# A masked update added to DRAM by accumulating transfers in the two cellular layers of a four-layer convolution kernel

## The chip, the cores and the metric

The kernel runs on one core of one Trainium2 chip. The metric is the device time of one execution in microseconds (us), lower is better. Three timed executions of the kernel before the change took 2888.09, 2889.95 and 2891.01 us; their median is 2889.95 us.

## The reference, cut to what matters

The input is 1024 samples of a 16 x 16 grid with 16 channels. Four layers follow each other, each of the form x = x + layer(groupnorm(x)). Layer 0 is a tensor-train product, layer 2 a 3 x 3 convolution. Layers 1 and 3, which the change touches, are one step of a cellular automaton:

```python
def update(x):                       # x is the normalized input
    xt = jnp.transpose(x, (0, 3, 2, 1))
    pre = _alive(xt)                 # channel 3, maximum over 3 x 3, > 0.1
    p = jnp.concatenate([xt, depthwise(xt, conv1), depthwise(xt, conv2)], axis=1)
    flat = p.reshape(B * W * Hh, 48)
    h = jax.nn.relu(flat @ fc0_w.T + fc0_b)          # 128 hidden values
    d = (h @ fc1_w.T + fc1_b).reshape(B, C, W, Hh)
    mask = (pre & _alive(d)).astype(xn.dtype)
    return jnp.transpose((xt + d) * mask, (0, 3, 2, 1))
x = x + update(_gn(x))               # _gn: group norm of 8 groups
```

So layers 1 and 3 need, for every element, x + (normalized x + d) * mask.

## The kernel before, in words

**Data.** The samples are worked on in two halves of 512 (n = 0 and 1). Two SBUF tiles, X0 and X1 (`XN`), hold one half each, as 128 partitions x 32 lines x 512 samples. Between layers a half lies in DRAM, in a tensor of its own per layer boundary: `xf[l][n]` (lines 117 to 122; `xf[3]` is another name of `xf[2]`).

**Passes.** A layer is done half by half. `layer_nca` (line 1461) is called four times, in this order on the chip: layer 1 half 0 (from 1662 us of the profile), layer 1 half 1 (from 1927 us), then, after the two convolution passes of layer 2, layer 3 half 0 (from 2376 us) and layer 3 half 1 (from 2627 us). I call these passes 1 to 4. While TensorE works on one half, VectorE normalizes the other half in the background (`norm_cw`, `norm_lines`: the lines 641, 649, 657, 669 and 682 in the profile).

**Inside a pass.** Both depthwise convolutions and the first matrix are folded into one product. One *row tile* is the 128 hidden values of one of 256 rows for 512 samples: several matmuls of 32 partitions into a PSUM bank `ph` (`tile_of_row`, line 1681, matmul on line 1704), then ScalarE's relu into an SBUF tile `hid` (line 1707). Four row tiles make a quad; two quads make one output tile of 128 partitions x 512 samples (`fc1`, line 1527, matmul on line 1534, PSUM bank `po`). There are 64 quads and 32 output tiles in a pass, eight output tiles in each of four quarters (q = 0 to 3). Then `finish` (line 1540) lets VectorE form u = po + bias + normalized x (line 1546), which also frees the bank `po`.

**Mask.** The mask is made in the first quarter alone, from flags of channel 3 (lines 1542 and 1564), by bf16 matmuls into two more banks (`pcnt`, line 1573) and two VectorE operations (lines 1578 and 1579). `masked` runs three slots after the `finish` of the following tile. In the later quarters the mask is there and `residual` (line 1583) follows `finish` directly.

**Residual.** `fetch` (line 1513) loads the old activations of the tile from DRAM into `r` on SyncE's DMA queue (SP). GpSimd (POOL) multiplies u by the mask (line 1587) and adds it to r (line 1588); for the last tile of a pass, and for tiles done in half width, VectorE does both. Seven slots later SP stores r to `xf[l + 1]` (line 1590). In pass 4 the sum is not stored but turned by TensorE (line 1598) and copied by VectorE into the output's layout.

**Order.** The order of instructions on every engine is the program's order. `plan` (line 1627) writes TensorE's order by hand, in slots. In a slot each of four groups of 32 partitions advances its own row tile by one matmul, so up to four matmuls run side by side; two quads that are complete take two slots. `room` (line 1636) lets a new row tile begin only if fewer than `BANKS` = 8 PSUM banks are taken in the plan; `pcnt` banks are not in that count, although they come from the same pool of eight (`nca_ps = dict(h=8)`, line 1857). `run` (line 1717) mixes loads and background steps between the slots. SBUF pools are given by `nca_sb` (line 1856): ten `hid` buffers, two of u, four of r.

Of the kernel before, what the change touches and what calls it, by code (L numbers as in the profile page):

```python
# [9 lines left out]
F32 = mybir.dt.float32  # L10
# [3 lines left out]
ALU = mybir.AluOpType  # L14
# [5 lines left out]
B, S, C = 1024, 16, 16  # L20
P = 128
NB = 512
NCH = B // NB
# [81 lines left out]
def conv_preact_kernel(ctx: ExitStack, tc: tile.TileContext, a: dict, out: bass.AP):  # L105
# [8 lines left out]

    XN = [big.tile([P, NL, NB], F32, tag=f"xn{i}", name=f"xn{i}") for i in range(2)]

    xf = [
        [dram.tile([8, 4, P, NB], F32, tag=f"xf{l}_{n}", name=f"xf{l}_{n}") for n in range(NCH)]
        for l in range(5)
    ]  # L120

    xf[3] = xf[2]

    xr = [dram.tile([2, S, P, NB], F32, tag=f"xr{n}", name=f"xr{n}") for n in range(NCH)]

# [762 lines left out]
    def tile_cw(t, i):  # L888

        return t[i % 8, i // 8]  # L890

    def rows_wc(t, wh, h, n=1):

        t = t[4 * wh : 4 * wh + 4].rearrange("w q (c h) b -> (w q c) h b", h=S)
        return t[:, h : h + n]
# [246 lines left out]
    def residual_steps(n, vs):  # L1142

        def add(w):
            G.dma_start(
                xf[1][n][w // 2].rearrange("q (c v h) b -> v (q c) h b", v=2, h=S)[w % 2],
                xr[n][w // 8, :, 16 * (w % 8) : 16 * (w % 8) + 16].rearrange("h f b -> f h b"),
                accum_op=ALU.add,
            )

        return [(1, lambda w=w: add(w)) for w in vs]

    def output_steps(n):

        steps = []

        lines = xf[4][n].rearrange("w q (c v h) b -> h (q c v) w b", v=2, h=S)

        def load(h, st):
            st["x"] = work([P, 8, P], "xs", "xs")
            for g in range(4):
                nc.sync.dma_start(st["x"][32 * g : 32 * g + 32], lines[h][:, :, P * g : P * g + P])

        def turn(h, st):
            st["o"] = work([P, 4, S, S], "xo", "xo")
            x = st["x"].rearrange("p w (j f) -> p f w j", f=4)
            for f in range(4):
                V.transpose(  # L1170
                    st["o"][:, f].rearrange("p (w v) c -> p w c v", v=2), x[:, f]
                )

        def store(h, st):
            nc.sync.dma_start(
                out[n * NB : n * NB + NB, h].rearrange("(p f) w c -> p f (w c)", f=4),
                st["o"].rearrange("p f w c -> p f (w c)"),
            )

        sts = [{} for _ in range(S)]  # L1180
        steps += [lambda: load(0, sts[0]), 4]
        for h in range(S):
            if h + 1 < S:
                steps.append((0, lambda h=h: load(h + 1, sts[h + 1])))
            steps += [lambda h=h: turn(h, sts[h]), (0, lambda h=h: store(h, sts[h]))]
        return steps
# [4 lines left out]
    def layer_train():  # L1191
# [78 lines left out]
        def tiles(t, a2, q, w):  # L1270

            return t[4 * a2 + w : 4 * a2 + w + 3 : 2, q].rearrange("w p b -> p w b")

        def store(u):
            ph, q, w = units[u]
            r = st["r", u]
            goes = OUTER[ph][1]
            if -1 in goes.values():
                neg = work([P, 2, NB], "t4", "neg")
                A.mul(neg, r, -1.0)  # L1280
            for (a2, n), sign in goes.items():
                first = all((a2, n) not in OUTER[j][1] for j in range(ph))
                src = r if sign > 0 else neg
                if first:
                    nc.sync.dma_start(tiles(xf[1][n], a2, q, w), src)
                else:
                    G.dma_start(tiles(xf[1][n], a2, q, w), src, accum_op=ALU.add)  # L1287

        def pieces(u, k):

# [73 lines left out]
    def layer_conv(X, n, other):  # L1364
# [75 lines left out]
        def finish(h):  # L1440

            if h == 0:
                G.tensor_copy(come, other[0:1, NL - 1, 0:1])
            for wh in range(2):
                r = work([P, NB], "r", "conv")
                A.activation(r, st["po", h][wh], AF.Identity, bias=b2)  # L1446
                G.dma_start(rows_wc(xf[2][n], wh, h), r.unsqueeze(1), accum_op=ALU.add)  # L1447

        steps = []
        for h in range(0, S, 2):  # L1450
# [10 lines left out]
    def layer_nca(X, n, l, L, xo=None):  # L1461
# [9 lines left out]
        def cols(hf):  # L1471
            return slice(0, NB) if hf is None else slice(hf * NB // 2, (hf + 1) * NB // 2)
# [39 lines left out]

        def fetch(i):
            r = st["r", *divmod(i, 8)] = work([P, NB], "r", "res1")
            nc.sync.dma_start(r, tile_cw(xf[l][n], i))

        def start():
            if n == 0 or l == 3:
# [8 lines left out]
        def fc1(q, w2, v, hf, hid):  # L1527
            if v == 0:
                st["po"] = bank([P, NB], "h", "po1")[:, width(hf)]
                if q > 0 and hf != 1:  # L1530
                    fetch(8 * q + w2)
            po = st["po"]
            for j in range(4):
                T.matmul(  # L1534
                    po[32 * j : 32 * j + 32], nca["w1"][:, v], hid[j], start=v == 0, stop=v == 1
                )
            if v == 1:
                finish(q, w2, hf, po)

        def finish(q, w2, hf, po):  # L1540
            if q == 0:
                V.tensor_scalar(
                    st["f", w2][64:96], po[96:128], nca["b1"][96:128], ALIVE, ALU.add, ALU.is_gt
                )
            u = st["u", q, w2] = work([P, NB], "u", "u")[:, width(hf)]
            V.scalar_tensor_tensor(u, po, nca["b1"], X[:, 8 * q + w2, cols(hf)], ALU.add, ALU.add)  # L1546
            if q > 0:
                residual(q, w2, hf)
                return

            ws = range(w2 - 1 if w2 else 0, 8 if w2 == 7 else w2)

            def masked():
                for w in ws:
                    mask(w)
                    residual(0, w)

            for w in ws:
                fetch(w)
            after(3, masked)  # L1560

        def flags(w2):
# [18 lines left out]
            )  # L1581

        def residual(q, w2, hf=None):
            u, r = st["u", q, w2], st["r", q, w2][:, cols(hf)]

            by = V if (q, w2) == (3, 7) or hf is not None else G
            by.tensor_tensor(u, u, st["m"][:, w2, cols(hf)], ALU.mult)  # L1587
            by.tensor_tensor(r, r, u, ALU.add)  # L1588
            if xo is None:
                after(7, lambda: nc.sync.dma_start(tile_cw(xf[l + 1][n], 8 * q + w2), r))  # L1590
            else:
                after(8 if hf is None else 4, lambda: turn(q, w2, r, hf))

        def turn(q, w2, r, hf):
            g0, n = (0, 4) if hf is None else (2 * hf, 2)
# [28 lines left out]
        def after(n, fn):  # L1624
            later.append((st["slot"] + n, fn))

        def plan():
# [6 lines left out]
            now, evacs, free_at, t, f = [None] * 4, 0.0, [], 0, 0  # L1634

            def room():
                return len(free_at) + sum(x is not None for x in now) < BANKS

            while f < len(quads):
                free_at = [b for b in free_at if b > t]  # L1640
# [110 lines left out]
    def put(L):  # L1751
        return lambda: nc.sync.dma_start(pack, L["pack"])
# [4 lines left out]
    def steps_of(*more):  # L1757
        return (lambda: None), [x for m in more for x in m]
# [14 lines left out]
    with ExitStack() as es:  # L1773
# [43 lines left out]
        def with_operand(i, step):  # L1817
# [31 lines left out]
        nst, N = parts_cw(X0, True, 3)  # L1849
        bg = alone(N, 0) + alone(N, 1) + alone(N, 2) + rstd(nst, slice(0, 96)) + [3] + scaled(N, range(3))  # L1850
        run(
            steps_of(phases[6]), 210, load_cw(X0, xf[1][0]) + [put(L1)], (bg, 0.12, 0.97), by=0.2
        )
    nst.clear()
    last = alone(N, 3) + rstd(nst, slice(96, 128)) + [3] + scaled(N, [3])
    nca_sb = dict(t4=2, s=3, n=2, wq=5, mask=1, f=5, hid=10, u=2, r=4, nx=1)
    nca_ps = dict(h=8)
    conv_sb, conv_ps = dict(gn, s=3, r=16, hx=2), dict(o=6, m=2)
    on_vector[0] = True
    with ExitStack() as es:  # L1860
        shared[0] = "h"
        stage(es, nca_sb, nca_ps)
        run(
            layer_nca(X0, 0, 1, L1), 250, load_cw(X1, xf[1][1]), (last, 0.0, 0.21),
            (norm_cw(X1, False), 0.23, 1.0), by=0.3,
        )
        run(
            layer_nca(X1, 1, 1, L1), 245, load_wc(X0, xf[2][0]), (norm_lines(X0, False), 0.2, 1.0), by=0.3
        )
    with ExitStack() as es:  # L1870
        shared[0] = "m"
        stage(es, conv_sb, conv_ps)
        (first0, main0), (first1, main1) = layer_conv(X0, 0, X1), layer_conv(X1, 1, X0)
        bg = norm_lines(X1)

        bg = bg[:-16] + woven(bg[-16:], *[(6 + i, copy) for i, copy in enumerate(first1)])
        run((lambda: now(first0), main0), 108, load_wc(X1, xf[2][1]), (bg, 0.09, 1.04), by=0.07)
        run(
            (lambda: None, main1), 108, load_cw(X0, xf[3][0]) + [put(L3)], (norm_cw(X0, True), 0.12, 1.06), by=0.07
        )  # L1880
    with ExitStack() as es:
        shared[0] = "h"
        stage(es, nca_sb, nca_ps)
        run(layer_nca(X0, 0, 3, L3), 245, load_cw(X1, xf[3][1]), (norm_cw(X1, False), 0.2, 1.0), by=0.3)
    with ExitStack() as es:
        stage(es, dict(nca_sb, xs=2, xo=2), nca_ps)

        xo = X0.rearrange("p n b -> p (n b)").rearrange("p (g h w c) -> p g h w c", g=4, h=S, w=S)
        run(layer_nca(X1, 1, 3, L3, xo), 280, (), (output_steps(0), 0.0, 0.93))
# [28 lines left out]
```

## Time and profile before

| what | value |
|---|---|
| three timed runs, median (lowest to highest) | 2889.95 us (2888.09 to 2891.01) |
| the profiled execution's own time | 2891.76 us |
| its span, from the first to the last instruction | 2890.1 us |
| TensorE (PE) busy | 2790.4 us, 97% of the span |
| VectorE (DVE) / ScalarE (ACT) / GpSimd (POOL) busy | 57% / 43% / 27% |
| pass 1, pass 2, pass 3, pass 4 begin | 1662, 1927, 2376, 2627 us |

The profile is one execution with every instruction's start and duration. A group of instructions is given by line, engine, operation and operands. "Idle before" is the time in which the engine stood still ahead of such an instruction, with the instruction whose end released it behind an arrow. PE is matmuls, PEld the loading of their weights, which overlaps them. Matmuls are pipelined, so a busy PE need not be at its peak. PEclk is the clock granted to TensorE as a share of the full one. TensorE takes an fp32 matmul as two records in the trace.

### The profile page before, as it was taken

What the parts mean: (1) busy time and instruction counts of PE and PEld (TensorE: products, weight loads), DVE (VectorE), ACT (ScalarE), POOL (GpSimd) and SP (SyncE); (2) the same over time, 40 slices, a digit from 0 to 9 for tenths busy, and PEclk for the clock granted to TensorE, in tenths of its full rate; (3) what the DMA queues carried; (4) which work ended last, traced back from release to release, by engine and by line L of the source; (5) the groups of instructions that cost most, each with busy time, mean ns of one, the idle gap of its engine ahead of it and who ended that gap; (6) DMA issues with size and microseconds to landing.
All of it is one profiled execution on the core that took longest, in us unless ns stands there. A gap on an engine that the chain in (4) does not pass through costs nothing.

```text
span 2890.1 us, 47471 instructions
## 1 busy us (share of the span) xinstructions
PE 2790.4 (97%) x19028; PEld 1831.6 (63%) x19028; DVE 1648.7 (57%) x1941; ACT 1237.2 (43%) x2168; POOL 773.4 (27%) x825
## 2 busy tenths in 40 slices
PE   5999999999999999999999999999999999999997
PEld 4777888877888888888888733333333334334443
DVE  7425744732644455444356568766977776857433
ACT  3243232124221211221122166676677666666664
POOL 1272010155012041000100015434542224443331
PEclk7899999999999999999999989999999999999998
DMA  6265744446485477363352154346447866444566
GB/s 231 82 128 182 255 131 140 125 78 155 116 221 103 91 179 178 77 156 63 81 142 38 22 168 155 123 139 208 133 127 183 194 93 224 135 127 123 146 191 214
DMA packets 261835, 408.58 MB, mean 141 GB/s; under 512 B 31828, under 2 KB 142984, under 8 KB 255472
## 3 DMA queue, kind: packets, MB, share of 16 engines
q1 hardware_dynamic: 209904, 301.70, 32.5%
q0 software_dynamic: 51520, 103.72, 19.7%
q8 instruction: 151, 2.47, 0.3%
q14 instruction: 68, 0.56, 0.1%
q10 hardware_dynamic: 192, 0.13, 0.0%
HBM read 236.48 MB, written 173.92 MB: 142 GB/s over the span
## 4 chain that ended last, share of the span: by engine, by line
PE 64%; issue 8%; DVE 8%; POOL 3%; DMA 1%; ACT 1%; SPq 0%; POOLq 0%; DVEq 0%; ACTq 0%
PE po L1303 37%; PE ph L1704 13%; PE po L1534 5%; PE pw L1233 3%; DVE xn L682 2%; PE po L1396 2%; DVE sq L669 1%; DVE sq L649 1%; DVE u L1546 1%; POOL xf L1447 1%; POOL res L1588 1%; POOL u L1587 1%; DMA xn<-xf 1%; PE ptx L1598 1%; PE po L1405 0%
## 5 line engine op out<-in xcount | busy, mean ns | idle before, releaser
L1303 PE MATMUL po<-xn,s 128*128 128x256 f32 x3584 | 813.0, 384 | 2.2 <-DVE s L1260 2.2
L1707 ACT ACTIVATE hid<-ph,pack 128x512 f32<-128x512 f32 (+1 forms) x1040 | 644.6, 683 | 346.7 <-PE ph L1704 201.5
L1303 PEld LDWEIGHTS po<-xn,s 128*128 128x128 f32 x3584 | 677.8, 191 | 112.6 <-issue 9.5
L1303 PE MATMUL po<-xn,w 128*128 128x256 f32 x2688 | 613.8, 383 | 2.1 <-DVE xn L1043 2.1
L1303 PEld LDWEIGHTS po<-xn,w 128*128 128x128 f32 x2688 | 505.5, 191 | 86.4 <-issue 11.1
L1704 PE MATMUL ph<-xn,wq 32*128 32x512 f32 (+1 forms) x3752 | 523.2, 593 | 16.8 <-DVE u L1546 16.6
L1235 ACT COPY w<-pw 128x512 f32<-128x512 f32 x448 | 230.0, 599 | 518.1 <-PE pw L1233 328.9
L1704 PEld LDWEIGHTS ph<-xn,wq 32*128 32x128 f32 x3752 | 230.4, 186 | 253.4 <-issue 207.7
L1260 DVE TENSOR_TENSOR s<-w 128x1024 f32<-128x1024 f32 x224 | 271.0, 1220 | 180.4 <-PE po L1303 180.3
L1587 POOL TENSOR_TENSOR u<-u,mask 128x512 f32<-128x512 f32 x123 | 185.3, 1506 | 571.0 <-DVE u L1546 355.0
L1704 PE MATMUL ph<-xn,pack 32*128 32x512 f32 x1288 | 284.4, 625 | 11.2 <-DVE u L1546 4.7
L1287 POOL DMA_DIRECT2D xf<-r x56 | 68.9, 1357 | 834.5 <-DVE r L1341 448.7
L1341 DVE TENSOR_TENSOR r<-r,po 128x512 f32<-128x512 f32 x168 | 115.1, 685 | 270.5 <-PE po L1303 250.8
L1534 PE MATMUL po<-hid,pack 128*32 128x512 f32 (+1 forms) x2080 | 261.0, 598 | 0.1
L682 DVE TENSOR_TENSOR xn<-xn,m 128x1024 f32<-128x1024 f32 x160 | 215.3, 1377 | 50.1 <-ACT m L705 49.9
L1347 ACT COPY r<-po 128x256 f32<-128x256 f32 x112 | 41.7, 372 | 456.6 <-PE po L1303 433.5
L1351 DVE TENSOR_TENSOR r<-r,po 128x256 f32<-128x256 f32 x112 | 47.1, 421 | 327.7 <-PE po L1303 327.7
L1588 POOL TENSOR_TENSOR res<-res,u 128x512 f32<-128x512 f32 x123 | 204.0, 1659 | 16.9 <-DMA res<-xf 6.3
L1546 DVE SCALAR_TENSOR_TENSOR u<-po,pack,xn 128x512 f32<-128x512 f32 (+1 forms) x130 | 96.0, 739 | 170.8 <-PE po L1534 155.5
L1704 PEld LDWEIGHTS ph<-xn,pack 32*128 32x128 f32 x1288 | 122.8, 188 | 102.2 <-issue 68.6
L1396 PE MATMUL po<-xn,convw 128*128 128x512 f32 x368 | 167.4, 608 | 6.0 <-ACT conv L1446 3.2
L1534 PEld LDWEIGHTS po<-hid,pack 128*32 128x32 f32 x2080 | 55.5, 109 | 178.2 <-issue 87.3
(190 smaller groups left out, 2460.5 us busy)
## 6 DMA issues: line engine op xcount, KB each, us to landing
xn<-xf SPq DMA_DIRECT2D x96, 512.0 KB, 6.1
wq<-L_conv_wy SPq DMA_DIRECT2D x192, 192.0 KB, 2.9
res<-xf SPq DMA_DIRECT2D x128, 256.0 KB, 3.2
gq<-g_dram SPq DMA_DIRECT2D x448, 64.0 KB, 2.9
xf<-r POOLq DMA_DIRECT2D x56, 512.0 KB, 7.0
xf<-res SPq DMA_DIRECT2D x96, 256.0 KB, 2.0
piece<-xb SPq DMA_DIRECT2D x32, 512.0 KB, 4.9
xf<-xr POOLq DMA_DIRECT2D x32, 512.0 KB, 11.5
```

The source lines that it names most:

```text
L682: V.tensor_tensor(part, part, m().unsqueeze(1).broadcast_to([P, 2, NB]), op)
L1235: A.copy(w.rearrange("p i b t m -> p (i b t) m")[:, :, 32 * r : 32 * r + 32].rearrange("p k (v o) -> p v k o", v=2), pw[r].rearrange("p v ...
L1260: V.tensor_tensor(t.rearrange("p i t m -> p i (t m)"), x, y, f)
L1303: T.matmul(po, matrix(u, what)[:, i, t], x, start=i == t == 0, stop=i == 1 and t == 3)
L1341: V.tensor_tensor(part, part, po.unsqueeze(1).broadcast_to([P, 2, 256]), ALU.add)
L1396: T.matmul(st["po", h][wh], conv["fw"][:, y], X[:, 16 * wh + h + y - 1], start=y == max(0, 1 - h), stop=y == min(2, S - h),)
L1534: T.matmul(po[32 * j : 32 * j + 32], nca["w1"][:, v], hid[j], start=v == 0, stop=v == 1)
L1546: V.scalar_tensor_tensor(u, po, nca["b1"], X[:, 8 * q + w2, cols(hf)], ALU.add, ALU.add)
L1587: by.tensor_tensor(u, u, st["m"][:, w2, cols(hf)], ALU.mult)
L1588: by.tensor_tensor(r, r, u, ALU.add)
L1704: T.matmul(ph, w, x, start=k == 0, stop=k == len(tiles) - 1)
L1707: A.activation(h, ph, AF.Relu, bias=nca["bt"][:, r : r + 1])
```

## The change

There is one DRAM tensor per half for the whole kernel, `xf[n]`, in place of one per layer boundary. In passes 1 to 3 the old activations are no longer fetched: VectorE multiplies u by the mask, and a DMA issued by GpSimd adds u to `xf[n]` in place (an accumulating transfer). GpSimd does no arithmetic in any pass: in pass 4 VectorE does the product and the sum. In passes 1 to 3 there are twelve `hid` buffers (ten before), four of u (two before) and none of r; pass 4 keeps its ten, two and four. In all four passes `plan` counts with seven banks while fewer than 16 quads are done, that is in the first quarter.

```diff
-    xf = [
-        [dram.tile([8, 4, P, NB], F32, tag=f"xf{l}_{n}", name=f"xf{l}_{n}") for n in range(NCH)]
-        for l in range(5)
-    ]
-
-    xf[3] = xf[2]
+    xf = [dram.tile([8, 4, P, NB], F32, tag=f"xf{n}", name=f"xf{n}") for n in range(NCH)]
...
         def fc1(q, w2, v, hf, hid):
...
-                if q > 0 and hf != 1:
+                if q > 0 and hf != 1 and xo is not None:
                     fetch(8 * q + w2)
...
-            for w in ws:
-                fetch(w)
+            if xo is not None:
+                for w in ws:
+                    fetch(w)
             after(3, masked)
...
         def residual(q, w2, hf=None):
-            u, r = st["u", q, w2], st["r", q, w2][:, cols(hf)]
-
-            by = V if (q, w2) == (3, 7) or hf is not None else G
-            by.tensor_tensor(u, u, st["m"][:, w2, cols(hf)], ALU.mult)
-            by.tensor_tensor(r, r, u, ALU.add)
+            u = st["u", q, w2]
+            V.tensor_tensor(u, u, st["m"][:, w2, cols(hf)], ALU.mult)
             if xo is None:
-                after(7, lambda: nc.sync.dma_start(tile_cw(xf[l + 1][n], 8 * q + w2), r))
-            else:
-                after(8 if hf is None else 4, lambda: turn(q, w2, r, hf))
+                G.dma_start(tile_cw(xf[n], 8 * q + w2), u, accum_op=ALU.add)
+                return
+            r = st["r", q, w2][:, cols(hf)]
+            V.tensor_tensor(r, r, u, ALU.add)
+            after(8 if hf is None else 4, lambda: turn(q, w2, r, hf))
...
             def room():
-                return len(free_at) + sum(x is not None for x in now) < BANKS
+                most = BANKS - (f < 16)
+                return len(free_at) + sum(x is not None for x in now) < most
...
-    nca_sb = dict(t4=2, s=3, n=2, wq=5, mask=1, f=5, hid=10, u=2, r=4, nx=1)
+    nca_sb = dict(t4=2, s=3, n=2, wq=5, mask=1, f=5, hid=12, u=4, nx=1)
...
-        stage(es, dict(nca_sb, xs=2, xo=2), nca_ps)
+        stage(es, dict(nca_sb, hid=10, u=2, r=4, xs=2, xo=2), nca_ps)
```

All other lines of the diff name `xf[n]` where they named `xf[1][n]` to `xf[4][n]`.

More of the change, by code (lines that the diff above doesn't have):

```diff
@@ L1145, in add @@
             G.dma_start(
[L1146 removed]
+                xf[n][w // 2].rearrange("q (c v h) b -> v (q c) h b", v=2, h=S)[w % 2],
                 xr[n][w // 8, :, 16 * (w % 8) : 16 * (w % 8) + 16].rearrange("h f b -> f h b"),
@@ L1155, in output_steps @@
         steps = []
-        lines = xf[4][n].rearrange("w q (c v h) b -> h (q c v) w b", v=2, h=S)
+        lines = xf[n].rearrange("w q (c v h) b -> h (q c v) w b", v=2, h=S)
         def load(h, st):
@@ L1284, in store @@
                 if first:
-                    nc.sync.dma_start(tiles(xf[1][n], a2, q, w), src)
+                    nc.sync.dma_start(tiles(xf[n], a2, q, w), src)
                 else:
-                    G.dma_start(tiles(xf[1][n], a2, q, w), src, accum_op=ALU.add)
+                    G.dma_start(tiles(xf[n], a2, q, w), src, accum_op=ALU.add)
         def pieces(u, k):
@@ L1446, in finish @@
                 A.activation(r, st["po", h][wh], AF.Identity, bias=b2)
-                G.dma_start(rows_wc(xf[2][n], wh, h), r.unsqueeze(1), accum_op=ALU.add)
+                G.dma_start(rows_wc(xf[n], wh, h), r.unsqueeze(1), accum_op=ALU.add)
         steps = []
@@ L1514, in fetch @@
             r = st["r", *divmod(i, 8)] = work([P, NB], "r", "res1")
-            nc.sync.dma_start(r, tile_cw(xf[l][n], i))
+            nc.sync.dma_start(r, tile_cw(xf[n], i))
         def start():
@@ L1851, in conv_preact_kernel @@
         run(
-            steps_of(phases[6]), 210, load_cw(X0, xf[1][0]) + [put(L1)], (bg, 0.12, 0.97), by=0.2
+            steps_of(phases[6]), 210, load_cw(X0, xf[0]) + [put(L1)], (bg, 0.12, 0.97), by=0.2
         )
@@ L1863, in conv_preact_kernel @@
         run(
-            layer_nca(X0, 0, 1, L1), 250, load_cw(X1, xf[1][1]), (last, 0.0, 0.21),
+            layer_nca(X0, 0, 1, L1), 250, load_cw(X1, xf[1]), (last, 0.0, 0.21),
             (norm_cw(X1, False), 0.23, 1.0), by=0.3,
@@ L1867, in conv_preact_kernel @@
         run(
-            layer_nca(X1, 1, 1, L1), 245, load_wc(X0, xf[2][0]), (norm_lines(X0, False), 0.2, 1.0), by=0.3
+            layer_nca(X1, 1, 1, L1), 245, load_wc(X0, xf[0]), (norm_lines(X0, False), 0.2, 1.0), by=0.3
         )
@@ L1876, in conv_preact_kernel @@
         bg = bg[:-16] + woven(bg[-16:], *[(6 + i, copy) for i, copy in enumerate(first1)])
-        run((lambda: now(first0), main0), 108, load_wc(X1, xf[2][1]), (bg, 0.09, 1.04), by=0.07)
+        run((lambda: now(first0), main0), 108, load_wc(X1, xf[1]), (bg, 0.09, 1.04), by=0.07)
         run(
-            (lambda: None, main1), 108, load_cw(X0, xf[3][0]) + [put(L3)], (norm_cw(X0, True), 0.12, 1.06), by=0.07
+            (lambda: None, main1), 108, load_cw(X0, xf[0]) + [put(L3)], (norm_cw(X0, True), 0.12, 1.06), by=0.07
         )
@@ L1883, in conv_preact_kernel @@
         stage(es, nca_sb, nca_ps)
-        run(layer_nca(X0, 0, 3, L3), 245, load_cw(X1, xf[3][1]), (norm_cw(X1, False), 0.2, 1.0), by=0.3)
+        run(layer_nca(X0, 0, 3, L3), 245, load_cw(X1, xf[1]), (norm_cw(X1, False), 0.2, 1.0), by=0.3)
     with ExitStack() as es:
-        stage(es, dict(nca_sb, xs=2, xo=2), nca_ps)
+        stage(es, dict(nca_sb, hid=10, u=2, r=4, xs=2, xo=2), nca_ps)
         xo = X0.rearrange("p n b -> p (n b)").rearrange("p (g h w c) -> p g h w c", g=4, h=S, w=S)
```

## The prediction

> **What bounds the kernel now.** I read four views in this order: the page's groups, the table of busy time by stretch (cut at the passes and at the end of each first quarter), the waits, and the timeline around the longest stalls.
>
> ```profile
> L1704 PE MATMUL ph<-xn,wq 32*128 32x512 f32 (+1 forms) x3752 | 523.2, 593 | 16.8 <-DVE u L1546 16.6
> L1587 POOL TENSOR_TENSOR u<-u,mask 128x512 f32<-128x512 f32 x123 | 185.3, 1506 | 571.0 <-DVE u L1546 355.0
> L1588 POOL TENSOR_TENSOR res<-res,u 128x512 f32<-128x512 f32 x123 | 204.0, 1659 | 16.9 <-DMA res<-xf 6.3
> ```
>
> ```profile
> core 0: us, PE busy (x) PEld busy (x) DVE busy (x) ACT busy (x) POOL busy (x), PEclk, DMA share, GB/s
> 1662.00:1740.00 78.00, 71.71 (x478) 29.12 (x476) 47.88 (x59) 47.65 (x77) 16.30 (x13) 0.89 0.52 163
> 1740.00:1928.00 188.00, 181.77 (x1474) 71.00 (x1472) 146.49 (x116) 122.08 (x196) 86.49 (x50) 0.99 0.42 132
> 1928.00:1985.00 57.00, 56.89 (x464) 24.82 (x456) 31.36 (x43) 42.54 (x71) 15.74 (x12) 1.00 0.68 227
> 1985.00:2161.00 176.00, 170.07 (x1432) 65.33 (x1432) 147.11 (x110) 119.65 (x190) 93.25 (x51) 1.00 0.45 141
> ...
> 2434.00:2626.00 192.00, 183.62 (x1470) 70.10 (x1464) 145.95 (x114) 122.84 (x196) 91.33 (x51) 0.98 0.42 130
> 2626.00:2688.00 62.00, 59.91 (x474) 26.36 (x478) 38.34 (x62) 41.66 (x69) 14.26 (x12) 1.00 0.48 133
> 2688.00:2872.00 184.00, 183.28 (x1660) 79.77 (x1652) 77.36 (x145) 121.15 (x203) 57.01 (x48) 1.00 0.60 171
> ```
>
> PE is busy nearly all the time in every pass: the kernel is bound by the PE's own stream of matmuls, and GpSimd's 389 us (185.3 + 204.0) lie beside it. Only what makes PE stand still, or lengthens its stream, moves the end. What makes it stand still is VectorE's queue (waits of the whole span):
>
> ```profile
> PEld ph L1704 <- DVE u L1546: 34.0, 22, 4.7
> PE ph L1704 <- DVE u L1546: 21.4, 18, 3.9
> DVE u L1546 <- POOL res L1588: 14.6, 15, 6.1
> ```
>
> PE waits for a bank that VectorE's u has to free, and VectorE comes late. The PE rows count; weight loads wait ahead of the same matmuls. Two more stalls are in the first quarter of pass 1, which takes 78 us against 57 in pass 2:
>
> ```profile
> 1705.31 3.35 DVE L728 RECIPROCAL r<-t 32x512 f32<-32x512 f32 x1
> ...
> 1711.65 0.69 DVE L1578 TENSOR_SCALAR mask<-pcnt 128x512 fp8e4<-128x512 f32 x1
> 1712.40 1.32 PE L1704 MATMUL ph<-xn,pack 32*128 32x512 f32 x6 [2.52 <-DVE mask L1578]
> ```
>
> The mask's VectorE operation stands behind a reciprocal and its Newton steps; PE waits until it frees a mask bank. After it, up to 1726, matmuls start 0.85 us apart in place of 0.43, and again from 1730.3 to 1733 after the second stall (3.5 us, for xn L682): the clock was halved.
>
> **What the Trainium skill says.** "SBUF — State Buffer", section "Who interferes with whom": a VectorE instruction with two SBUF inputs contends with a GpSimd instruction that reads SBUF, one with at most one does not. The trace agrees: L1546, one of whose inputs is PSUM, takes 0.75 us everywhere, while L649, two SBUF inputs, means 1.70 us in the late quarters of passes 1 and 2 and 1.22 in the convolution, where GpSimd only issues DMAs. "TensorE: Matmul & The Clock Gate", section "What's actually happening": an idle window of about 3.4 us halves PE's clock. The trace agrees in kind: the doubled spacing follows the stalls of 2.5 to 4.5 us, not the shorter ones. "DMA: Bandwidth & Descriptors", section "Anatomy of one DMA — SWDGE (gpsimd) path": about 2.0 us plus bytes / 436e3, an estimate of 2.6 us for 256 KB. The accumulating DMAs of the convolution (L1447, same size) show 5.7 us median, up to 11.7; I use those.
>
> **The change, part by part.**
>
> *GpSimd's arithmetic goes.* What it gives is VectorE's undisturbed speed. Excess over 1.22 us in the late quarters, pass 1: L682 31 x (1.45 - 1.22) = 7.2, L649 20 x 0.48 = 9.5, L669 16 x 0.43 = 6.9, L641 4 x 0.93 = 3.7, together 27 us; pass 2 likewise 31, pass 3 29.
>
> *The products move to VectorE:* 0.69 us each (L1587 on DVE, full width), 24 of the late quarters and two masked late, 26 x 0.69 = 18 us per pass. So VectorE's 146 us of 188 become about 137: relief, but a modest one. For the PE stalls it matters what lies between two u's. Longest one in pass 3: between u at 2485.96 and u at 2494.52 lie five background operations, 8.0 us now, 6.1 undisturbed, plus 0.69: the stall of 4.0 becomes 2.8. Likewise 2.6 at 1749.6 becomes 1.2 (2.8 saved, two products added), and 1.5 at 1836, 2.2 at 2032 and 1.7 at 1854 become 0, 0 and 0.7. Of these 12.0 us 4.7 stay, so 60% go. The PE rows of this wait in the three late stretches are 6.2 + 5.6 + 7.8 = 19.6: **12 us saved**. Next late is VectorE's own background work.
>
> *Pass ends.* The first convolution matmul waits 2.8 us for u of pass 2, and pass 4's first 1.8. Three L682 ahead of that u take 5.45, undisturbed 3.65: 1.8 saved, 0.8 at the other, and one half-clock window of 3.4 us (1.7 lost) behind the first: **4 us**. Half-clock windows after the stalls at 1750 and 2435: 1.5 each, **2.5 of it saved**.
>
> *First quarter of pass 1.* 78 - 57 = 21, less 3 of norm matmuls (mean, variance, spread about 1 us each), leaves 17 that a stall-free quarter would save: 2.7 + 3.5 stalls, the rest the halved clock and small waits. One bank less in the plan leaves more room for the mask banks; u no longer waits for GpSimd (14.6 us over all, 3.7 here); twelve `hid` let ScalarE go on to the copy m ahead of the second stall (it stood 5.3 us for a `hid` buffer). But the reciprocal stays ahead of the mask, and 7 + 2 banks are still nine of eight. Bounds 0 and 17; I take **10**.
>
> *One bank less.* By plan's own rule, walked through with the limit at 8 and at 7, the first quarter has 55 slots in place of 52 and the second 60 in place of 59. A slot of two times four matmuls is 0.86 us (48 records in 5.36 us on the chain), so 4 x 0.86 = 3.4 us a pass, **13.7 us lost** in four. Passes 2 and 4 wait for almost nothing in their first quarter (PE 56.89 of 57, 59.91 of 62), so nothing there pays it back; lower bound 10, if mask matmuls fit into the thinner slots.
>
> *Twelve `hid` elsewhere.* ACT waits 131 us for PE to free `hid`, but PE hardly waits for ACT (0.8 us before an fc1, while matmuls still run): 0. If that cover were gone, it would be up to 32 x 0.8 a pass.
>
> *Transfers.* 96 fetches and 96 stores of 256 KB leave SP's queue; 96 accumulating ones join GpSimd's, about 0.92 us each (L1447's median), 88 us in place of 300. Loads of weights and xn behind them on SP come earlier, which nobody waits for. A u buffer is held 0.69 + 0.92 + 5.7, at worst some 14 us; four last 4 x 7.3 = 29. On GpSimd itself the memset and the `come` copy at the start of the convolution now stand behind the last issues: ready near 2167, needed at 2170.6. Pass 4's output load needs pass 3's last transfer (2626.5 + 0.7 + 0.75 + 5.7 = 2634, now issued at 2630.8), and SP's nx loads are behind it, used at 2639: 0 to 2 us. All of this: 0, with -2 to +6 for the unknown.
>
> *Pass 4.* VectorE takes 28 x 1.38 = 39 us more, on 116 of 246: hidden. But it now waits in order for the fetched r. Tile 10's r lands 4.9 us after u would be ready (2718.4 against 2713.5), three others 0.5 to 2: copies behind it are late, PE's transposes wait there already. **1 us lost**, bounds 0 and 6.
>
> *Sum.* -12 - 4 - 2.5 - 10 + 13.7 + 1 = **-13.8 us**. Against the profiled execution: span 2890.1 to 2876.3, and with the 1.7 us around it 2891.8 to 2878. The median of the timed runs is 1.8 below that execution: **2876**.
>
> **Rivals.**
>
> *All stalls go* (chance 0.22). The whole queue shifts forward once VectorE catches up: 19.6 + 17 + 6 + 3 = 46 saved, 10 to 14 lost: about -34, **2856**. For it: the stalls come from backlog, and backlog adds up. Against: the five operations between two u's stay.
>
> *They cancel* (0.16). Pass 1's first quarter keeps its stall, since the reciprocal stays: 4 fewer saved stall and no clock back, about -4: **2886**. It would show as PEclk near 0.9 there.
>
> *Slower: the plan's slots* (0.14). Place: the first quarter of each pass; mechanism: PE's written order is four slots longer where it was not waiting. Price 13.7 us, sure. It decides as soon as less than 8 us of stalls are won back: if the products on VectorE delay masks and u's as much as GpSimd did (0.69 for each tile in the same queue, against 1.22 in place of 1.7 on few operations). With 4 won back and 2 lost in pass 4: +12, **2902**. Against: passes 1 to 3 have 20 us of u waits alone.
>
> *The change doesn't do what it says:* GpSimd's arithmetic could remain only by an error in the code; no weight.
>
> **How the numbers follow.** Chances: forecast 0.48 (2866 to 2884), all stalls go 0.22, cancel 0.16, slower 0.14. A difference of 0.2%, 5.8 us, is about what a measurement of this kernel can tell from no change, so the border is 2884 and 2896. Faster: 0.48 + 0.22 + a little of the third, 0.72; same 0.15; slower 0.13. The range reaches down to the middle of the second case and up to the border of the fourth, 2854 to 2896, which leaves out about 2 in 10.
>
> **What would show it.** Right: L649 and L682 at 1.22 in all passes, no row of L1587 on POOL; the wait of PE for u L1546 down by half or more; pass 1's first quarter near 68 us with PEclk above 0.95; the first quarters of passes 2 and 4 about 3 us longer. Wrong: L649 still over 1.5, or first quarters that do not grow, or a new row in which PE or DVE waits for a DMA.

## The result and the profile after

The kernel after takes 2883.39 us (median of 11 runs, 2880.95 to 2885.87), beside 2890.15 us for the kernel before in the same session (11 runs, 2888.09 to 2892.46): a ratio of 0.9975, 95% interval 0.9966 to 0.9985. It is faster, by 6.8 us. The profiled execution has a span of 2884.2 us. "Late" stands below for quarters 2 to 4 of a pass.

By stage, from the starts of the passes in the two traces. Each column is one profiled execution:

| stage | before, us | after, us | difference |
|---|---|---|---|
| all ahead of pass 1 (code not changed) | 1662.3 | 1666.1 | +3.8 |
| pass 1: first quarter / late | 75.4 / 190.0 | 73.8 / 185.5 | -1.6 / -4.5 |
| pass 2: first quarter / late | 54.5 / 178.5 | 56.0 / 170.7 | +1.5 / -7.8 |
| convolution, to the start of pass 3 | 215.3 | 211.5 | -3.8 |
| pass 3: first quarter / late | 55.7 / 193.8 | 57.0 / 181.2 | +1.3 / -12.6 |
| pass 4: first quarter / late | 59.8 / 185.0 | 63.0 / 201.1 | +3.2 / +16.1 |

A gap of 1.8 us ahead of pass 4 is gone as well. Passes 1 to 3 and the convolution win 27.5 us, and pass 4 gives 19.3 back. The 3.8 us ahead of pass 1 are chance: over all profiles of this study pass 1 begins between 1662.0 and 1667.7 us, and the order has nothing to do with the edits. Pass 1 itself varies, too: in E1 and E2 below, whose code is the same up to pass 4, it takes 262.4 and 259.3 us beside 259.2 here. So the 6.1 us of pass 1 are not far outside chance, and its first quarter, 73.8 us here, takes 77.0 in E1. Passes 2 and 3 repeat to 0.1 us between these three.

The groups of the kernel after; u is now formed on line 1541, the matmul of `ph` is line 1700, the product line 1581, the accumulating transfer line 1583 and pass 4's sum line 1586:

```profile
L1700 PE MATMUL ph<-xn,wq 32*128 32x512 f32 (+1 forms) x3752 | 520.4, 593 | 10.0 <-DVE xn L155 4.7 <-DVE u L1541 4.7 <-PE ph L1700 0.4
L677 DVE TENSOR_TENSOR xn<-xn,m 128x1024 f32<-128x1024 f32 x160 | 189.4, 1219 | 34.4 <-ACT m L700 34.1
L1581 DVE TENSOR_TENSOR u<-u,mask 128x512 f32<-128x512 f32 (+1 forms) x130 | 88.9, 684 | 4.5
L1583 POOL DMA_DIRECT2D xf<-u x96 | 82.7, 861 | 642.3 <-DVE u L1581 620.4 <-DMA nx<-xn 12.4 <-DVE s1s L652 7.1
```

PE's idle time ahead of these matmuls fell from 16.8 to 10.0 us, and only 4.7 of it is for u; but a new releaser, `xn L155`, stands in it with 4.7. L677 runs at 1.22 us throughout (1.38 before). The product is 0.68 us on VectorE; GpSimd only issues, 0.86 us a transfer. The same table of busy time by stretch as before:

```profile
core 0: us, PE busy (x) PEld busy (x) DVE busy (x) ACT busy (x) POOL busy (x), PEclk, DMA share, GB/s
1666.00:1740.00 74.00, 66.67 (x449) 26.19 (x450) 50.83 (x63) 46.46 (x74) 5.54 (x6) 0.91 0.54 150
1740.00:1925.00 185.00, 182.14 (x1496) 69.90 (x1496) 134.61 (x143) 122.87 (x198) 22.36 (x26) 0.99 0.53 115
1925.00:1981.00 56.00, 55.80 (x433) 22.48 (x432) 31.00 (x45) 41.00 (x67) 5.16 (x6) 1.00 0.55 145
1981.00:2152.00 171.00, 170.09 (x1468) 66.39 (x1464) 133.33 (x139) 118.85 (x191) 22.39 (x26) 1.00 0.58 128
...
2602.00:2665.00 63.00, 61.20 (x451) 25.50 (x445) 41.65 (x67) 40.82 (x67) 0.88 (x1) 1.00 0.50 133
2665.00:2866.00 201.00, 194.02 (x1677) 88.19 (x1675) 113.18 (x199) 122.90 (x205) 0.00 (x0) 0.98 0.54 155
```

In the late stretches of passes 1 and 2 PE is nearly without a gap (182.1 of 185, 170.1 of 171), and VectorE has 12 to 14 us less to do than before. The first stretch is still at PEclk 0.91: stretches at half clock (PEclk 0.50) make 13.6 us of it, where they made 17.1 us before (and 20.5 in E1). The last is new: 201 us, with VectorE at 113 in place of 77. The waits of the whole span:

```profile
PE ph L1700 <- DVE u L1541: 11.4, 9, 3.2
PEld ph L1700 <- DVE u L1541: 9.5, 8, 3.0
DVE res L1586 <- DMA res<-xf: 7.3, 3, 6.1
PE ph L1700 <- DVE xn L155: 5.7, 4, 4.4
```

PE's waits for u fell from 21.4 to 11.4 us. The last two lines were not there before: VectorE waits for the fetched activations, and PE then waits for VectorE. In the first quarter of pass 1 the timeline shows where the stall went:

```profile
1710.29 3.35 DVE L723 RECIPROCAL r<-t 32x512 f32<-32x512 f32 x1
...
1717.09 0.75 DVE L1541 SCALAR_TENSOR_TENSOR u<-po,pack,xn 128x512 f32<-128x512 f32 x1
1717.87 0.42 DVE L1560 TENSOR_SCALAR flags<-xn 32x512 bf16<-32x512 f32 x1
...
1717.98 2.04 PE L1700 MATMUL ph<-xn,pack 32*128 32x512 f32 x2 [3.18 <-DVE u L1541]
```

The reciprocal and the four operations of its Newton step now hold a u, where they held a mask operation before: another victim, and a stall of 3.18 us where it was 2.52. A second one, also for u, takes 2.1 us at 1694.8. And the late part of pass 4:

```profile
2816.68 2.70 SPq L1159 DMA_DIRECT2D xs<-xf  x4
...
2819.43 0.45 SPq L1510 DMA_DIRECT2D res<-xf  x1
...
2823.55 0.69 DVE L1586 TENSOR_TENSOR res<-res,u 128x512 f32<-128x512 f32 x1 [6.14 <-DMA res<-xf]
2824.16 1.00 DVE L155 COPY xn<-ptx 128x256 f32<-128x256 f32 x2
...
2825.31 3.10 PE L1700 MATMUL ph<-xn,wq 32*128 32x512 f32 x10 [4.36 <-DVE xn L155]
...
2828.34 3.64 PE L1529 MATMUL po<-hid,pack 128*32 128x512 f32 x16
```

The fetch is issued behind four loads of `xs` on SP. VectorE's sum waits 6.14 us for it, the copy of the transposed output behind the sum is late, so PE lacks a bank for 4.36 us; then, at half clock, sixteen fc1 matmuls take 3.64 us, where they took 1.92 at 2813.95. GpSimd met late fetches in the kernel before as well (6.3 us in all on its row of sums, one of 4.6), and PE waited 0.2 us for its sums in pass 4.

### The profile page after: what moved, and what is told of

It is laid out like the page before. It is cut to its first block, busy times and chain, and to the rows that moved or that the text cites. A ratio compares the mean times of both kernels' runs of the same rounds, so it can differ in the third digit from the quotient of the medians.

```text
span 2884.2 us, 47182 instructions
## 1 busy us (share of the span) xinstructions
PE 2793.3 (97%) x19028; PEld 1833.6 (64%) x19028; DVE 1650.8 (57%) x2091; ACT 1235.1 (43%) x2168; POOL 466.9 (16%) x675
## 4 chain that ended last, share of the span: by engine, by line
PE 68%; issue 6%; DVE 5%; DMA 2%; ACT 1%; POOL 1%; SPq 0%; POOLq 0%; DVEq 0%; ACTq 0%
PE po L1298 37%; PE ph L1700 15%; PE po L1529 6%; PE pw L1228 3%; PE po L1391 3%; DMA xn<-xf 1%; DVE xn L677 1%; DVE sq L644 1%; PE po L1400 1%; POOL xf L1583 1%; PE ptx L1593 1%; DVE u L1541 1%; PE pcnt L1569 0%; DVE u L1581 0%; PE L_conv_pe L390 0%
## 5 line engine op out<-in xcount | busy, mean ns | idle before, releaser
L1255 DVE TENSOR_TENSOR s<-w 128x1024 f32<-128x1024 f32 x224 | 271.3, 1221 | 182.1 <-PE po L1298 182.1
L1336 DVE TENSOR_TENSOR r<-r,po 128x512 f32<-128x512 f32 x168 | 115.3, 686 | 269.3 <-PE po L1298 249.5
L1529 PE MATMUL po<-hid,pack 128*32 128x512 f32 (+1 forms) x2080 | 263.3, 599 | 0.7 <-ACT hid L1703 0.5
L677 DVE TENSOR_TENSOR xn<-xn,m 128x1024 f32<-128x1024 f32 x160 | 189.4, 1219 | 34.4 <-ACT m L700 34.1
L1583 POOL DMA_DIRECT2D xf<-u x96 | 82.7, 861 | 642.3 <-DVE u L1581 620.4
L1228 PE MATMUL pw<-R,gq 32*128 32x128 f32 x3584 | 136.7, 285 | 16.0 <-DMA gq<-g_dram 15.5
```

The lines of the kernel that those rows point to most:

```text
L677: V.tensor_tensor(part, part, m().unsqueeze(1).broadcast_to([P, 2, NB]), op)
L1228: T.matmul(pw[r][:, v, i], g[rows, 2 * v + i], R[rows], start=True, stop=True)
L1255: V.tensor_tensor(t.rearrange("p i t m -> p i (t m)"), x, y, f)
L1336: V.tensor_tensor(part, part, po.unsqueeze(1).broadcast_to([P, 2, 256]), ALU.add)
L1529: T.matmul(po[32 * j : 32 * j + 32], nca["w1"][:, v], hid[j], start=v == 0, stop=v == 1)
L1583: G.dma_start(tile_cw(xf[n], 8 * q + w2), u, accum_op=ALU.add)
```

## The experiments

Theory A, from the result: undisturbed VectorE and a shorter VectorE queue win in passes 1 to 3; the bank reserve and pass 4's arithmetic on VectorE give most of it back. Rivals put the loss on `hid`, on the transfers, or the gain on the traffic that is gone. Ratios are to the kernel before, measured in the same session (its medians there lie between 2889.95 and 2891.13 us); E1 to E4, E5 to E8, E10 to E12 and E13 are a session each, so most differences to the kernel after are between sessions. Stage lengths come from one profiled execution of each. There is no E9.

**E1. Pass 4's product and sum back on GpSimd** (from the kernel after).

```diff
-            V.tensor_tensor(u, u, st["m"][:, w2, cols(hf)], ALU.mult)
+            by = G if xo is not None and hf is None and (q, w2) != (3, 7) else V
+            by.tensor_tensor(u, u, st["m"][:, w2, cols(hf)], ALU.mult)
...
-            V.tensor_tensor(r, r, u, ALU.add)
+            by.tensor_tensor(r, r, u, ALU.add)
```

> Pass 4's product and sum go back to GpSimd, all else as in the changed kernel. Theory (VectorE's queue in pass 4, with the late fetch in it, gives back what passes 1 to 3 won): pass 4 falls from 264 us to about 248 (its 245 before plus three to four slots), the VectorE waits for the fetched r vanish, and the time falls from 2883.4 to about 2867. Rival (the four planned slots and chance stalls made pass 4 long): pass 4 stays at 260 or more, 2880.

Measured: 2871.59 us, ratio 0.9937 (0.9925 to 0.995), 11.8 us below the kernel after. Pass 4 takes 250.3 us in place of 264.2; passes 2 and 3 are the same to 0.1 us, and pass 1 is the 3.2 us longer that are named above as chance. So pass 4's arithmetic costs 12 to 14 us where it was put. The late fetch is still there, and GpSimd meets it:

```profile
POOL res L1587 <- DMA res<-xf: 5.9, 3, 5.4
```

PE waits 1.0 us for it, at the transposes of that sum, and for no bank.

**E2. Only pass 4's fetch moved from SP to GpSimd's queue** (from the kernel after).

```diff
-            nc.sync.dma_start(r, tile_cw(xf[n], i))
+            G.dma_start(r, tile_cw(xf[n], i))
```

> Only the 32 fetches of pass 4 move from SP's queue to GpSimd's, which is otherwise idle there; VectorE keeps the product and the sum. If the late fetch behind SP's other transfers is what hurts, VectorE's 7.3 us of waits for r and the stall of 5 us with its halved clock go: about -9 us, 2874, pass 4 near 255. If the two more operations ahead of the output copies are what hurts, nearly nothing: 2881 to 2884.

Measured: 2879.44 us, ratio 0.9962 (0.995 to 0.9975), 4 us below the kernel after; pass 4 256.4 us, its last quarter 64.4 in place of 72.6. In this profile VectorE waits for no fetched r. So the late fetch is 7.8 of the 13.9 us in the profile, more than the 4 us between the medians: the profiled execution of the kernel after was the slowest of its eleven. The other 6 lie over all quarters (1.3 to 2.1 each over E1), where two operations more stand in VectorE's order; by which path they cost PE time is not shown.

**E3. Eight banks in the first quarter again** (from the kernel after).

```diff
-                most = BANKS - (f < 16)
+                most = BANKS
```

> The plan counts eight banks in the first quarter again, all else as in the changed kernel. My prediction's price says 13.7 us less, 2870. What the first quarters of passes 2 and 3 show (1.4 us longer each) and that of pass 4 (3.2) says about 5 to 7 less, 2877. Rival: the spare bank is needed for the masks now that VectorE also has the products, and the first quarters get longer: 2884 to 2890.

Measured: 2870.05 us, ratio 0.9933 (0.9919 to 0.9946): the reserve costs 13.3 us. But not evenly: pass 1 becomes 12.0 us shorter, pass 2 2.8, pass 4 3.7, pass 3 3.6 longer. The first quarter of pass 1 falls from 73.8 to 65.3 us, at PEclk 1.00 throughout. PE's two long waits for u there (2.1 and 3.2 us) are gone; it waits 1.1 us for a mask and 2.8 for L677's xn. So the two stalls of the kernel after and their half clock came with the reserve; the reciprocal is in VectorE's order in both, here ahead of a mask again.

**E4. Ten `hid` in place of twelve** (from the kernel after).

```diff
-    nca_sb = dict(t4=2, s=3, n=2, wq=5, mask=1, f=5, hid=12, u=4, nx=1)
+    nca_sb = dict(t4=2, s=3, n=2, wq=5, mask=1, f=5, hid=10, u=4, nx=1)
```

> Ten hid buffers in passes 1 to 3 in place of twelve. My prediction's term of 0: 2883, no difference. Rival (ScalarE's waits for a free hid buffer hold PSUM banks and so the PE): the late quarters of passes 1 to 3 grow by 3 us each or more, 2890 or over.

Measured: 2888.96 us (13 runs), ratio 1.0 (0.9992 to 1.0008): 5.6 us over the kernel after. The first quarters grow, by 6.0, 2.2 and 2.2 us in passes 1 to 3; the late ones stay. Of the 6.0 only 2.7 are over E1, which has twelve `hid` and the same 20 us of half clock there. The 5.6 us between the medians are most of the 6.8 us that the change wins.

**E5. E1 and E3 together.**

> The first and the third experiment together: eight banks in the plan, product and sum of pass 4 on GpSimd. If the slots and VectorE's queue in pass 4 are separate losses, they add: 2883.4 - 11.8 - 13.3 = 2858. If pass 4's part of the second is the same time counted twice, 2864.

Measured: 2856.26 us, ratio 0.988 (0.9866 to 0.9893). The two losses add up: 11.8 + 13.3 = 25.1 of the 27.1 us between the kernel after and this one. Pass 4 is 244.9 us, to a tenth that of the kernel before.

**E6. E3, and of pass 4 only the sum on GpSimd.**

```diff
-            V.tensor_tensor(r, r, u, ALU.add)
+            by = V if (q, w2) == (3, 7) or hf is not None else G
+            by.tensor_tensor(r, r, u, ALU.add)
```

> Eight banks; in pass 4 VectorE does the product and GpSimd the sum, so that GpSimd and not VectorE waits for the fetched r. If the wait in VectorE's order is most of pass 4's loss: as the run with both on GpSimd, within 3 us (2858 to 2861). If any operation of VectorE ahead of the output copies costs its time: half of the 6 us that pass 4 still lost with a punctual fetch, and GpSimd's reads beside it: 2862 to 2866.

Measured: 2851.51 us, ratio 0.9874 (0.9857 to 0.9892). Pass 4 takes 246.2 us. The product on VectorE costs it 1.3 us, so what hurt was the sum, the operation that waits for the fetch. On GpSimd one sum, at 2674.2, begins 5.2 us after its product was ready, and the pass hardly notices. Of the 6 us that E2's pass 4 still lost without a late fetch, some 5 are then the sum's (an estimate, 6.1 less 1.3). The time is below E5's although pass 4 is not: in the profile pass 1 begins 5.7 us earlier here, and passes 1 and 3, whose code is the same, are 2.8 and 1.7 us shorter. That is chance.

**E7. Product and sum of passes 1 to 3 on VectorE, with fetches, stores and all buffers as before** (from the kernel before).

```diff
-            by = V if (q, w2) == (3, 7) or hf is not None else G
+            by = V if xo is None or (q, w2) == (3, 7) or hf is not None else G
```

> The kernel before, with product and sum of passes 1 to 3 on VectorE; fetches, stores, ten hid and two u buffers and eight banks stay as before, pass 4 is untouched. If undisturbed VectorE operations are the gain of passes 1 to 3, most of it is here without an accumulating transfer: 2.76 us less per tile on GpSimd, 1.38 more on VectorE, against some 30 us less of disturbance: 2870 to 2880. If taking the sum out of VectorE's queue (the accumulating transfer) or the deeper u and hid are the gain: 2887 to 2895.

Measured: 2884.82 us (21 runs), ratio 0.9977 (0.997 to 0.9984). That is 5.8 us below the kernel before, between the two ranges expected. L682 means 1.218 us, undisturbed, and yet passes 1 to 3 take 263.3, 232.4 and 250.2 us, 2 us less in sum than before (265.4, 233.0, 249.5). The rest of the gain stands in the convolution (209.6 in place of 215.3), where E11 has it too without any of this. VectorE's sums wait only 3.1 us in all for their fetches, so late fetches do not hide a gain. To be undisturbed, at the price of both operations, is next to no gain in these passes. The half of theory A that I had built the forecast on falls.

**E8. E5 with the product of passes 1 to 3 on GpSimd as well**: only the sum is left to the transfer.

```diff
-            by = G if xo is not None and hf is None and (q, w2) != (3, 7) else V
+            by = G if hf is None and (q, w2) != (3, 7) else V
```

> As the run with eight banks and pass 4 on GpSimd, but the product of passes 1 to 3 is GpSimd's too; the sum stays with the accumulating transfer. VectorE has 22 us a pass less to do than with the product, but GpSimd reads SBUF 1.1 to 2 us a tile beside it. If the disturbance is what counts: VectorE's two-input operations mean over 1.3 us again and passes 1 to 3 get 2 to 6 us longer each, 2864 to 2875. If the length of VectorE's queue counts: 3 us shorter each, 2850.

Measured: 2850.52 us, ratio 0.9862 (0.9849 to 0.9875), the lowest median of all, though not apart from E6's (2851.51): 39.6 us below the kernel before and 32.9 below the kernel after. GpSimd multiplies again and VectorE is disturbed again, yet the passes are 246.8, 223.8 and 241.0 us, neither longer nor 3 us shorter than in E3 and E6, where VectorE multiplies (247.2, 224.0 and 241.8 or 240.1; E5's pass 1, 250.0, is the long one of the three with this code). So the time came out as the second reading had it, but its reason did not: who multiplies makes no difference here. The groups of this kernel:

```profile
L677 DVE TENSOR_TENSOR xn<-xn,m 128x1024 f32<-128x1024 f32 x160 | 201.4, 1291 | 52.9 <-ACT m L700 52.7
L1582 POOL TENSOR_TENSOR u<-u,mask 128x512 f32<-128x512 f32 x123 | 182.7, 1485 | 589.8 <-DVE u L1541 396.2 <-DVE mask L1575 180.5 <-DMA xs<-xf 10.0
```

L677 means 1.29 us, between 1.22 and the 1.38 of before. What the two kernels' VectorE has to do in the late quarters of passes 1 to 3 goes with this: E7 has as much as before, E8 less. First E7, then E8, by stretch as above:

```profile
1738.00:1930.00 192.00, 186.27 (x1498) 72.52 (x1494) 153.41 (x170) 123.88 (x199) 0.00 (x0) 0.99 0.42 130
1984.00:2162.00 178.00, 173.53 (x1454) 66.63 (x1454) 150.23 (x163) 120.98 (x192) 0.31 (x1) 0.99 0.46 144
2427.00:2622.00 195.00, 186.62 (x1490) 70.43 (x1486) 149.88 (x167) 124.38 (x199) 0.00 (x0) 0.97 0.43 131
```

```profile
1730.00:1911.00 181.00, 180.28 (x1491) 70.05 (x1486) 131.37 (x118) 121.06 (x197) 63.15 (x52) 1.00 0.54 117
1966.00:2135.00 169.00, 168.41 (x1455) 65.24 (x1447) 132.68 (x112) 118.03 (x190) 67.43 (x52) 1.00 0.59 131
2402.00:2588.00 186.00, 182.74 (x1495) 70.38 (x1490) 131.61 (x116) 121.88 (x197) 66.23 (x52) 0.99 0.48 97
```

| kernel | VectorE busy there, us | length of these stretches, us |
|---|---|---|
| E7 | 453.5 | 565 |
| before | 444.9 | 563 |
| E5 | 401.4 | 539 |
| after | 400.8 | 538 |
| E8 | 395.7 | 536 |
| E12 (below: load as E8, two u) | 392.3 | 553 |
| E13 (below: load as E8, four u) | 395.0 | 539 |

E7's load is back where it was, made of added operations in place of disturbance, and so is its time. In after, E5 and E8 the load is 44 to 49 us less and the time 24 to 27. But they have more buffers too, and the last two rows part the two: less load with two u gives 10 us of it in these stretches (and loses much more in the first quarters, see E12), four u the other 14.

**E10. E5 with the old ten `hid` and two u.**

```diff
-    nca_sb = dict(t4=2, s=3, n=2, wq=5, mask=1, f=5, hid=12, u=4, nx=1)
+    nca_sb = dict(t4=2, s=3, n=2, wq=5, mask=1, f=5, hid=10, u=2, nx=1)
```

> As the run with eight banks and pass 4 on GpSimd (2856), but ten hid and two u buffers in passes 1 to 3. If the gain of passes 1 to 3 is that the sum has left the engines: 2856 to 2861. If it is the deeper hid and u: the passes go back towards the kernel before, 2870 to 2885. With two u buffers VectorE waits for the accumulating transfer of the tile before last, 4.2 us from issue to landing, which a tile's 7 us should hide outside the first quarter.

Measured: 2927.59 us, ratio 1.0128 (1.0115 to 1.0142), 71 us over E5, slower than before, and outside both ranges expected. The first quarters take 85.6, 74.1 and 74.7 us. Waits, then one case on the timeline:

```profile
DVE u L1541 <- DMA xf<-u: 49.5, 19, 6.7
PE ph L1701 <- DVE u L1541: 39.8, 18, 5.7
```

```profile
1698.05 0.75 DVE L1541 SCALAR_TENSOR_TENSOR u<-po,pack,xn 128x512 f32<-128x512 f32 x1 [3.99 <-DMA xf<-u]
...
1698.86 0.60 PE L1569 MATMUL pcnt<-flags,alive_w 32*128 32x512 bf16 x1 [4.45 <-DVE u L1541]
```

VectorE waits 3.99 us until the transfer that reads its buffer has landed, and PE 4.45 us for the bank that this u frees.

**E11. The bank reserve alone** (from the kernel before; the edit of E3 the other way round).

> The kernel before with seven banks in the plan of the first quarters and nothing else. My prediction's price, four slots a pass: 13.7 us more, 2904. If the reserve helps pass 1 as I assumed (10 us of its first quarter): 2894. If what eight banks won back in the changed kernel holds here too (12 us in pass 1, 2 to 4 in the others): 2904 to 2909.

Measured: 2906.36 us, ratio 1.0051 (1.0038 to 1.0065), 15 us slower: what E3 gave, from the other side. Passes 1, 2 and 4 are 7.3, 4.2 and 5.9 us longer, pass 3 1.0 shorter. The convolution is 5.6 us shorter, 209.7: the wait of 2.8 us for the last u of pass 2 ahead of it is gone, and so are two stretches of half clock, though GpSimd does all its arithmetic. So the 3.8 us that the convolution is shorter in the kernel after can't be put down to a relieved VectorE.

**E12. E8 with ten `hid` and two u** (the edit of E10).

> The smallest step from the kernel before: the product stays on GpSimd everywhere, hid ten, u two, eight banks, pass 4 as before; only the sum of passes 1 to 3 goes from GpSimd to the accumulating transfer, with fetch and store. If taking the sum off the engines is the gain: within 5 us of the runs with all parts, 2850 to 2858. If VectorE had to be rid of GpSimd's reads altogether, or needs the deeper buffers: half the gain or less, 2870 or more.

Measured: 2941.77 us, ratio 1.0184 (1.017 to 1.0198): the sum by transfers alone, without the buffers, makes the kernel 51 us slower, though VectorE has only 392.3 us to do in the late quarters. The first quarters take 89.2, 82.4 and 82.0 us, and VectorE waits for its own source buffers:

```profile
DVE u L1541 <- DMA xf<-u: 64.6, 20, 6.7
```

E10 and E12 move the same bytes as E5 and E8. So the traffic that is gone is not enough for a gain; what it adds to one is not shown.

**E13. E8 with ten `hid` and four u.**

```diff
-    nca_sb = dict(t4=2, s=3, n=2, wq=5, mask=1, f=5, hid=12, u=4, nx=1)
+    nca_sb = dict(t4=2, s=3, n=2, wq=5, mask=1, f=5, hid=10, u=4, nx=1)
```

> As the run with the sum alone moved (2942), but four u buffers; hid stays ten, the product on GpSimd, eight banks, pass 4 as before. If the u buffers, held by the accumulating transfer, were all that the run with two of them lacked: 2851 to 2857, as with twelve hid. If hid is needed too: 2858 to 2880, with the first quarters longer by 2 us or more.

Measured: 2857.43 us, ratio 0.9888 (0.9872 to 0.9905), at the border of the two ranges. Two more u are worth 84 us over E12. Twelve `hid` are worth the other 7 to E8 at most: in the profiles, whose spans differ by 3.3 us only, E8's passes 1 to 3 are 5.3 us shorter, 2.9 of them in the first quarter of pass 1, where chance alone makes 3.

**What stays open.** Four u without the accumulating transfers were not run. Shown is that the sum by transfers loses with two u and wins with four; how much four u would win by themselves is not. In E7 VectorE waits only 0.8 us for a u that GpSimd still holds, against 14.6 before, and the late quarters don't shorten; that speaks against a large part, but E7's load is 9 us higher, so it doesn't settle it.

## Why the prediction was right or wrong

The median, 2883.4, lies 7.4 us above the forecast and in the range; the direction is right. By its steps:

- **Late-quarter waits for u, -12, half-clock windows, -2.5, pass ends, -4.** The waits went, and the size was too small: the late quarters of passes 1 to 3 gave 24.9 us. PE's waits for u in them fell from 19.6 to 4.7 us, and the half clock from 10.2 to 3.4, worth some 3.4 us (an estimate, half of the difference). The other 6 or 7 us lie where PE counts as busy; a weight load that waits for u beside running matmuls does not show there (PEld's waits for u fell from 34.0 to 9.5 us over the whole span), and I had left those rows out of the sum. Whether they are the whole of it is not shown. The load of VectorE was forecast at 137 us a pass and became 134.6. At the pass ends the two waits are gone and the convolution is 3.8 us shorter, but E11 loses the first of these waits too, with GpSimd at work: that part may be luck.
- **GpSimd's arithmetic goes.** The step says that it "gives VectorE's undisturbed speed", and this was to pay for the product. Here the forecast had the cause of its largest term wrong. Undisturbed speed only pays for operations that come over (E7: VectorE 453.5 us busy in the late quarters, 444.9 before), and the product may as well stay on GpSimd (E8). The relief comes from the sum, which no engine carries any more, together with more u (E12 and E13); what the four u would give alone is open.
- **First quarter of pass 1, -10, less 3.4 of slots.** Measured -1.6 (in E1 +1.6) in place of -6.6. The failed part is "one bank less in the plan leaves more room for the mask banks": with eight banks the quarter is 8.5 us shorter, 10.1 below the kernel before, with PEclk at 1.00 (E3). So the 10 us and the returned clock were there to be had, without the reserve and with the reciprocal in its place. With the reserve PEclk stayed at 0.91, where above 0.95 was to show the step right. The part on twelve `hid` holds, for 2.7 to 6.0 us (E4). The two stalls that I put at 2.7 and 3.5 us stand in the trace at 2.5 and 2.8.
- **One bank less, +13.7.** Right in sum, from both sides (13.3 in E3, 15 in E11). Wrong in place: 3.4 a pass was the rule, but pass 1 had most, through stalls and half clock, and pass 3 lost nothing (3.6 us longer without the reserve in E3, 1.0 shorter with it in E11). The sum is in part luck.
- **Twelve `hid` elsewhere, 0.** Wrong by 4.4: 2.2 us in each first quarter of passes 2 and 3 (E4). I had read ACT's waits as cover, over whole passes, where the first quarters should have been read alone.
- **Transfers, 0.** Right as built: no engine waits for `xf<-u`. SP's queue does, 21.3 us ahead of pass 4's first output load, and the loads of nx behind it cost PE's weight loads 1.2 us, within the 0 to 2 of the forecast. But the estimate that "four last 29 us" was the load-bearing number: with two u the kernel is 84 us slower (E12 against E13).
- **Pass 4, +1, with bounds 0 and 6.** The step that failed worst. Beside the slots it cost 13.9 us in the profile (264.2 against E1's 250.3). I took the old landing times of the fetches, 4.9 us late for one tile; in the new order one came 6.1 us late, and its cost was not the wait alone but the copies behind it, PE's stall and then doubled matmul times. The new row in which VectorE waits for a DMA, named as a sign of being wrong, came. "39 us more on VectorE: hidden" was wrong as well: about 6 us of it showed with no fetch late (E2), and the product alone costs 1.3 (E6).

So the net came out near because two errors met, which is luck: passes 1 to 3 won more than I forecast, and pass 4 lost more. Of the rivals, "they cancel" (2886) was nearer in number than the forecast, and its sign, PEclk near 0.9 in the first quarter of pass 1, came true; but the stall was kept by the reserve (E3), not by the reciprocal alone, and the rest of its sum did not hold. The one that ended slower had the right price for the slots. "All stalls go" counted 46 us of gain ahead of the losses, the forecast 28.5; without the two losses the change gives 34 (E5), between them and nearer to the forecast.

## What to carry to other kernels

Before an operation moves to an in-order engine, list what it waits for and who needs what stands behind it: here a sum that waits for a DMA did little harm on GpSimd (E1, E6), and its late fetch cost some 8 us on VectorE (E2). If an accumulating transfer takes over a sum, its source is held until it has landed, so count buffers first. Undisturbed speed of one engine was no gain by itself here: compare what it saves with what the engine has to take over, in the stretch that matters.

## What the runs showed of the hardware that was not expected

An accumulating transfer of 256 KB from SBUF to DRAM took 4.2 us (median, issue to landing), after 0.86 us of issue on GpSimd:

```profile
xf<-u POOLq DMA_DIRECT2D x96, 256.0 KB, 4.2
```

The forecast used the convolution's 5.7 us. The Trainium skill, "DMA: Bandwidth & Descriptors", section "Anatomy of one DMA — SWDGE (gpsimd) path", has a formula that gives an estimate of 2.6 us; the measurement decides, and it lies between. After the stall of 4.36 us in pass 4 the clock was halved for 6.8 us, and sixteen fc1 matmuls took 3.64 us in place of 1.92. The prediction read that half clock follows stalls of 2.5 to 4.5 us and not shorter ones. That was too simple: the trace of the kernel before has it behind waits of 1.25 us (at 2435.7) and 2.1 us (at 2231.8), and not behind one of 2.0 us (at 2034.7). How long it lasts differs between executions of the same code, too: behind the stall of 3.2 us in the first quarter of pass 1 it was 6.8 us in the kernel after and 13.6 in E1, which is the 3.2 us by which E1's quarter is longer. So a small difference between two profiles can be the clock and not the edit.
